# Issuing the prefix products of batch 6 behind the last batch's output projection in the scan stage

## The chip, the cores and the metric

The kernel runs on one core of one Trainium2 chip. The metric is the device time of one execution in microseconds (us); "before" is the median of three runs. Times inside the execution are counted from the start of the span, the stretch from the program's first to its last instruction in the profile.

## What is computed

A block of four residual layers over x of 8 batches x 512 tokens x 256 features, in float32:

```
x = x + scan(layernorm(x))        # silu(x Win), decayed running sum over tokens, times Wout
x = x + ffn(layernorm(x))         # 16 experts, 4 chosen per token, plus 2 shared experts
x = x + attention(layernorm(x))   # 16 heads, causal, scores clipped
x = x + ffn(layernorm(x))         # same weights as the first ffn
```

In `ffn` each token picks 2 of 4 groups of experts and then 4 experts; only these are weighed into its output. The shared experts are computed for every token.

## The kernel before, in words

The kernel works in four stages. A *stretch* (L1315) computes scan or attention for one batch after the other and, beside it, what the following ffn can do early: the layer norm and routing of the batch before, the sorted scatter of its rows to memory, and the shared experts of the batch two back. After a stretch, `routed` (L826) goes through the sorted rows in blocks of 128. There are two stretches and two routed stages: scan, routed, attention, routed. The change touches the first stretch.

**The last iteration of a stretch**, b = 7, runs these pieces side by side (L1379 to L1426):

- `main(7)` (L498): four input projections with the scan (L506 to L522), then the output projection `add_projection` (L452). Its matmuls (L460) come in two halves of two 128-token tiles. Each half fills one bank of the accumulator memory PSUM (`py`), and one VectorE addition (L469) adds it to x. This text calls them half 0 and half 1. Each has 8 matmuls, which the profile shows as 16, since it splits a float32 product into two entries.
- six of the twelve steps of the shared experts of batch 5 (L1031 to L1051); their rest, and the experts of batches 6 and 7, come after the iteration.
- the sends of batch 5: sixteen indirect DMAs from GpSimd (L726), each of which scatters one tile of rows.
- the routing of batch 6, `Route(6)`: normalised rows (L443), their transposes (L403), the logits (L598, moved to SBUF by VectorE at L609), and then the generator `choices` (L621). This yields step by step: group scores, groups, the best four of two tiles, of the other two, and the chosen set `sel` (L668). Then come the *prefix products* (L676 and L677): two small matmuls of `sel` with a triangle and with ones, which count for each token the earlier tokens with the same expert. VectorE adds them to the running counts (`row`, L681, and `where`, L687). The next step makes the *places* of the rows (L693, L699). The one after it makes their *gains* (L709 to L712), which complete batch 6's rows. After that each step is one send (L726); before every second send ScalarE casts two places to integers (L723).

**The order of issue.** `timed(steps, *places)` (L362) gives each step of a piece a place between 0 and 1, and `beside` (L346) always takes the next step of the piece that is least far. `main(7)` counts 10240 columns: its four projections run at 0 to 0.3, and the four tiles of the output projection are issued at 0.6 and 0.7 (half 0) and at 0.8 and 0.9 (half 1). Half 0's addition is issued at 0.8, half 1's at 1.0. Behind this stands a scheduler: it takes the issue order as priority and arranges each engine's instructions by its own model of time. It can let a later instruction pass an earlier one that isn't ready by that model. An engine then runs its instructions in that fixed order, and a waiting instruction holds what is behind it. `tc.issue_after` and `tc.keep_in_program_order` pin single instructions. For batch 6, L675 pins the prefix products behind the last matmul of the six expert steps. The rows of batch 7 (L443) are pinned behind batch 6's gains (L441, L578, L712).

**After the iteration** (L1436 to L1455) follow the rest of batch 5's experts, batch 6's and batch 7's, the other twelve sends of batch 6, and the whole routing of batch 7. That routing needs x of batch 7 after half 1's addition. The counts of batch 7 follow from those of batch 6 (`counts`, L679 to L682). `blocks` (L740) makes the table of blocks. `routed` opens with an `If` (L1012), at which all engines meet.

Of the kernel before, what the change touches and what calls it, by code (L numbers as in the profile page):

```python
# [61 lines left out]
SENT = 4  # L62
# [18 lines left out]
def tile_hybrid_block(  # L81
# [257 lines left out]
    def behind(*pieces):  # L339
        def steps():  # L340
            for piece in pieces:
                yield from piece.steps

        return Piece(sum(piece.columns for piece in pieces), steps())

    def beside(*pieces):  # L346


        def steps():
            done = dict.fromkeys(range(len(pieces)), 0)  # L350
            while done:
                k = min(done, key=lambda k: done[k] / pieces[k].columns)
                step = next(pieces[k].steps, None)
                if step is None:
                    del done[k]
                else:
                    done[k] += step
                    yield step

        return Piece(sum(piece.columns for piece in pieces), steps())  # L360

    def timed(steps, *places):  # L362


        def scaled():
            now = 0
            for place in places:
                yield place - now
                now = place
                next(steps)  # L370
            for _ in steps:
                pass

        return Piece(1, scaled())

    def spread(first: float, last: float, many: int):
        return [first + (last - first) * k / many for k in range(many)]

    def some(steps, many: int):

        for _ in range(many):
            yield next(steps)

    def issue(piece):
        for _ in piece.steps:
            pass
# [85 lines left out]
    class Scan:  # L472
# [3 lines left out]

        norms, scores, choose = (0.08, 0.2, 0.32, 0.4), (0.48, 0.52, 0.61, 0.66), (0.71, 0.97)
        last_rows, last_scores = (0.26, 0.33), (0.43, 0.46)

        def load(self, b: int):  # L480
            if b + 1 < B and b > 0:
                with tc.issue_after(load_x(b + 1).ins):
                    for load in later[b - 1 :: shares]:
                        load()

        def end(self):
            pass
# [598 lines left out]
    class Attention:  # L1086
        mixture, ahead, copies = 1, 2, by_both
        early = 2
        norms, scores, choose = (0.0, 0.12, 0.2, 0.28), (0.42, 0.46, 0.55, 0.6), (0.66, 0.95)
        last_rows, last_scores = (0.2, 0.28), (0.35, 0.38)  # L1090

        def end(self):
            for e in range(first_expert, E):
# [221 lines left out]
    def stretch(layer):  # L1315
# [5 lines left out]
        def norm(b: int, first: bool = False):  # L1321
            def place():
                xn[b] = kb4(f"xn_{i}_{b}")
                return xn[b]

            return normed(b, f"l{i}_{b}", place, first, first)

        def turn(b: int, copies=layer.copies):
            return turned(lambda: xn.pop(b), f"l{i}_{b}", lambda xnT: xT.update({b: xnT}), copies)

        def project(b: int):
            made[b], piece = layer.project(b, xT.pop(b))
            return piece
# [4 lines left out]
        def experts(b: int):  # L1338
            return shared_experts(i, b, lambda: routes.pop(b).held["xnT"], i == 1)
# [31 lines left out]
        def start_route(b: int):  # L1371
            routes[b] = Route(i, b, layer.copies)
            store(b)
            return routes[b]
# [4 lines left out]
        for b in range(1 if begun else 0, B):  # L1379
            pieces = [begun or layer.main(b, made.pop(b))]  # L1380
            begun = None
            nxt, last = b + layer.ahead, b == B - 1
            fill = []
            if layer.ahead > 1 and not last:
                fill.append(project(b + 1))
            if b > 1:
                shared_sum = experts(b - 2)
                if last:

                    each = shared_sum.columns // 12  # L1390
                    rest = Piece((12 - HELD) * each, shared_sum.steps)

                    many = HELD * each if layer.mixture else HELD * each * 3 // 2
                    shared_sum = Piece(many, some(shared_sum.steps, HELD))
                fill.append(shared_sum)
                pieces.append(timed(sends.pop(), 0.1, 0.14, 0.18, *spread(0.22, 0.66 if last else 0.86, NT * TK)))
            if fill:
                pieces.append(behind(*fill))
            if b > 0:
                r = start_route(b - 1)  # L1400
                if last:
                    pieces.append(timed(r.norm(), *spread(0.0, 0.12, NT), *spread(*layer.last_rows, NT)))
                else:
                    first, then, rows, full = layer.norms
                    pieces.append(timed(r.norm(), *spread(first, then, NT), *spread(rows, full, NT)))
                sends.append(r.rest)
                if last:
                    pieces += [
                        timed(r.scores(), *layer.last_scores, *spread(0.5, 0.56, NT)),
                        timed(some(r.rest, PICKS), *spread(0.57, 0.67, PICKS - 1), 0.76),  # L1410
                        timed(some(r.rest, 3 + SENT), 0.79, 0.81, 0.83, *spread(0.85, 1.0, SENT)),
                    ]
                else:
                    pieces += [
                        timed(r.scores(), *layer.scores[:2], *spread(*layer.scores[2:], NT)),
                        timed(some(r.rest, PICKS), *spread(*layer.choose, PICKS)),
                    ]
            if nxt < B:
                added = layer.load(nxt)
                if added is not None:  # L1420
                    pieces.append(timed(added, 0.24, 0.28))
                pieces += [
                    timed(norm(nxt), *spread(0.32, 0.44, NT), *spread(0.56, 0.64, NT)),
                    timed(turn(nxt), 0.75, 0.79),
                ]
            issue(beside(*pieces))  # L1426
            if layer.ahead == 1 and nxt < B:
                issue(project(nxt))
            if i == 0 and b == 2:
                for make in pending:  # L1430
                    make()
# [4 lines left out]
        r = start_route(B - 1)  # L1436
# [20 lines left out]
    with banks_of(one=8):  # L1457
        table = stretch(Scan())
        wqkv_sb, wo_sb = load_attention_weights()
# [6 lines left out]
    with banks_of(one=4, pair=2):  # L1466
        table = stretch(Attention())
# [128 lines left out]
```

## Time and profile before

| what | value |
|---|---|
| median of three runs | 1713.41 us (1713.23, 1713.41, 1718.89) |
| the profiled execution, its own time | 1717.61 us |
| its span | 1715.9 us |
| mean granted TensorE clock | 0.976 |
| TensorE matmul busy | 1612.4 us, 94% of the span |
| VectorE, ScalarE, GpSimd busy | 1146.0, 758.0, 759.9 us |

The page gives busy time by engine (PE is TensorE's matmuls, PEld its weight loads, DVE VectorE, ACT ScalarE, POOL GpSimd, SP the DMA-issuing SyncE). The timeline shows each instruction with its start, its length, and, in brackets, how long its engine stood idle before it and what ended that. "remote" there means a semaphore was raised, but by nothing that the view could name. The ends of matmuls are modelled, not observed. The first routed stage begins at about 367 us, the attention stretch ends at about 1306 us.

### The profile page before, as it was taken

How to read it: one execution, taken by the hardware profiler on the slowest of the kernel's cores; microseconds unless marked ns; L12 is line 12 of the kernel's file. 1: busy time of each engine (PE TensorE's matmuls, PEld its weight loads, DVE VectorE, ACT ScalarE, POOL GpSimd, SP SyncE). 2: the span in 40 equal slices, each digit the busy share in tenths (PEclk: the TensorE clock that was granted, in tenths of full speed). 3: DMA queues.
4: the chain of work that ended last, by engine and by line, in shares of the span. 5: the costliest groups of instructions: out<-in, count | busy, mean ns of one | idle time of the engine just before them, and what ended most of it. 6: DMA issues, size and time to landing. Idle time of an engine off the chain costs nothing.

```text
span 1715.9 us, 34382 instructions
## 1 busy us (share of the span) xinstructions
PE 1612.4 (94%) x10092; PEld 1166.6 (68%) x10092; DVE 1146.0 (67%) x3681; ACT 758.0 (44%) x1506; POOL 759.9 (44%) x656
## 2 busy tenths in 40 slices
PE   6899996999999999999999999999897999999994
PEld 3566663569999999964345445444456999999993
DVE  7977876445666766657877777767753666666663
ACT  3223222135555555545554354454313555555552
POOL 3355553535555655530021431422451555555563
PEclk8999998999999999999999999999998999999997
DMA  4354321547776766540021121122543766677776
GB/s 162 129 180 165 135 96 69 168 104 108 108 104 96 119 103 100 78 93 13 26 70 57 64 80 59 52 75 70 178 159 83 107 96 101 96 138 129 129 127 178
DMA packets 247215, 180.38 MB, mean 105 GB/s; under 512 B 141456, under 2 KB 228272, under 8 KB 247024
## 3 DMA queue, kind: packets, MB, share of 16 engines
q1 hardware_dynamic: 193232, 102.09, 23.5%
q0 software_dynamic: 51984, 72.09, 23.4%
q10 hardware_dynamic: 1808, 3.93, 0.6%
q8 instruction: 86, 1.41, 0.3%
q14 instruction: 105, 0.86, 0.2%
HBM read 81.06 MB, written 96.94 MB: 104 GB/s over the span
## 4 chain that ended last, share of the span: by engine, by line
PE 42%; DVE 6%; DMA 2%; issue 1%; POOL 1%; ACT 1%; ACTq 0%; POOLq 0%; DVEq 0%
PE ph L924 15%; PE pyr L955 7%; PE ps_a L1169 5%; PE po_a L1204 3%; PE pg_m L1031 3%; PE pq_a L1114 3%; PE pd_m L1060 2%; PE py_a L460 2%; PE pv_a L1132 2%; DMA xg<-sorted_m,slots_m 1%; POOL xg L726 1%; DVE w_all L1183 1%; PE pt L906 1%; DVE w_all L1191 1%; DMA part<-rows 1%
## 5 line engine op out<-in xcount | busy, mean ns | idle before, releaser
L965 POOL DMA_INDIRECT part<-rows x272 | 425.6, 1565 | 353.1 <-ACT rows L964 217.0
L726 POOL DMA_INDIRECT xg<-sorted_m,slots_m x256 | 260.1, 1016 | 338.7 <-ACT slots_m L723 84.8
L924 PEld LDWEIGHTS ph<-rows,gate 128*128 128x128 f32 x2160 | 279.1, 192 | 29.3 <-ACT rows L907 17.1
L924 PE MATMUL ph<-rows,gate 128*128 128x128 f32 x2160 | 291.6, 278 | 0.0
L924 PE MATMUL ph<-rows,up 128*128 128x128 f32 x2160 | 285.7, 275 | 0.0
L955 PE MATMUL pyr<-w_all,rows 128*128 x1088 | 278.9, 380 | 0.0
L924 PEld LDWEIGHTS ph<-rows,up 128*128 128x128 f32 x2160 | 263.3, 192 | 0.0
L897 DVE COPY up<-w_all 128x512 f32 x270 | 118.1, 438 | 217.3 <-PE ph L924 188.1
L897 ACT COPY gate<-w_all 128x512 f32 x270 | 166.7, 619 | 115.5 <-DVE up L897 53.6
L955 PEld LDWEIGHTS pyr<-w_all,rows 128*128 128x128 f32 x1088 | 187.0, 192 | 14.4
L964 ACT ACTIVATE rows<-pyr,gain 128x256 f32<-128x256 f32 x272 | 129.0, 474 | 80.2 <-PE pyr L955 58.2
L932 ACT ACTIVATE rows<-ph 128x256 f32<-128x256 f32 x272 | 104.7, 385 | 120.2 <-PE ph L924 100.5
L1180 ACT ACTIVATE w_all<-ps_a 128x1024 f32<-128x1024 f32 x128 | 124.4, 1021 | 57.6 <-PE ps_a L1169 48.2
L934 DVE TENSOR_TENSOR rows<-ph,rows 128x256 f32<-128x256 f32 x272 | 115.2, 423 | 43.8 <-ACT rows L932 37.1
L935 DVE TENSOR_TENSOR rows<-ph,rows 128x256 f32<-128x256 f32 x272 | 115.3, 424 | 26.0 <-issue 1.3
L1031 PE MATMUL pg_m<-xT_m,su_sb 128*128 128x512 f32 x256 | 126.9, 618 | 5.3 <-ACT expert_b L806 5.2
L1169 PE MATMUL ps_a<-w_all 32*128 32x384 f32 (+3 forms) x1024 | 123.0, 478 | 9.0 <-ACT w_all L1180 5.9
L1031 PE MATMUL pg_m<-xT_m,sg_sb 128*128 128x512 f32 x256 | 123.5, 604 | 1.0 <-issue 0.7
L1060 PE MATMUL pd_m<-sd_sb,act_m 128*128 128x256 f32 x512 | 121.4, 382 | 0.9 <-DVE act_m L1051 0.6
L1060 PEld LDWEIGHTS pd_m<-sd_sb,act_m 128*128 128x128 f32 x512 | 95.6, 190 | 25.1 <-issue 7.0
L1169 PEld LDWEIGHTS ps_a<-w_all 32*128 32x128 f32 x1024 | 48.8, 187 | 72.2 <-issue 30.1
L1031 PEld LDWEIGHTS pg_m<-xT_m,su_sb 128*128 128x128 f32 x256 | 46.5, 193 | 64.1 <-issue 51.6
(220 smaller groups left out, 2077.1 us busy)
## 6 DMA issues: line engine op xcount, KB each, us to landing
rows<-xg SPq DMA_DIRECT2D x712, 32.0 KB
rows<-xg SPq DMA_DIRECT2D x94, 134.0 KB
part<-x SPq DMA_DIRECT2D x16, 512.0 KB
part<-ys_m SPq DMA_DIRECT2D x14, 512.0 KB
sum<-part SPq DMA_DIRECT2D x13, 512.0 KB
w_all<-in_L_ffn_gate_w_dram SPq DMA_DIRECT2D x24, 256.0 KB
w_all<-in_L_ffn_up_w_dram SPq DMA_DIRECT2D x24, 256.0 KB
w_all<-in_L_ffn_down_w_dram SPq DMA_DIRECT2D x24, 256.0 KB
```

The costliest lines, as they stand in the source:

```text
L726: nc.gpsimd.indirect_dma_start(out=xg[i], out_offset=bass.IndirectOffsetOnAxis(ap=slots[:, at : at + 1], axis=0), in_=rows[:, t, :], in_of ...
L897: copy(here, w_all[:, bass.ds(held[n][0] + half * KD * F, KD * F)])
L924: nc.tensor.matmul(ph[s][:, f * P : (f + 1) * P], lhsT=both[s][:, k * F + f * P : k * F + (f + 1) * P], rhs=rows[:, ROW + k * P : ROW + (k ...
L934: nc.vector.tensor_mul(act, ph[0], act)
L935: made = nc.vector.tensor_mul(act, ph[1], act)
L955: nc.tensor.matmul(py, lhsT=act[:, f * P : (f + 1) * P], rhs=w_all[:, bass.ds(w + 2 * KD * F + f * D, D)], start=(f == 0), stop=(f == KF - 1),
L964: nc.scalar.mul(y, py, gain[:, TK : TK + 1])
L965: nc.gpsimd.indirect_dma_start(out=parts[i][n % 2], out_offset=bass.IndirectOffsetOnAxis(ap=rows[:, D + 2 * TK : D + 2 * TK + 1].bitcast(U ...
L1031: made = nc.tensor.matmul(dst, lhsT=w[:, k, f * P : (f + 1) * P], rhs=xnT[:, k, :], start=(k == 0), stop=(k == KD - 1),)
L1060: nc.tensor.matmul(py[:, j, :], lhsT=acts[n][:, f, t * P : (t + 1) * P], rhs=shared[n][3][:, f, :], start=(n == 0 and f == 0), stop=(n == ...
L1169: nc.tensor.matmul(ps[j // 2][:, j % 2, col : col + n], lhsT=k_sb[w][r, o, c * P : (c + 1) * P], rhs=q_sb[r, o, c * P : T], start=True, st ...
L1180: nc.scalar.activation(es[two], ps[two][:, :, 0:cols], AF.Exp, scale=ATT_SCALE)
```

## The change

Four places of steps are moved, in the scan stretch alone. The attention stretch gets the same places as before, now from a class attribute.

```diff
 class Scan:
         last_rows, last_scores = (0.26, 0.33), (0.43, 0.46)
+        last_places, last_sends = (0.91, 0.92, 0.93), 0.95
 class Attention:
         last_rows, last_scores = (0.2, 0.28), (0.35, 0.38)
+        last_places, last_sends = (0.79, 0.81, 0.83), 0.85
 stretch, if last:
-                        timed(some(r.rest, 3 + SENT), 0.79, 0.81, 0.83, *spread(0.85, 1.0, SENT)),
+                        timed(some(r.rest, 3 + SENT), *layer.last_places, *spread(layer.last_sends, 1.0, SENT)),
```

For batch 6 in the scan stretch the prefix products go from 0.79 to 0.91, the places from 0.81 to 0.92, the gains from 0.83 to 0.93, and the first four sends with their two casts from 0.85, 0.8875, 0.925 and 0.9625 to 0.95, 0.9625, 0.975 and 0.9875. The step before, which makes `sel`, stays at 0.76. In the issue order the prefix products thus come behind all matmuls of half 1 (0.8 and 0.9). No instruction is added or taken away.

## Prediction

> **What bounds the kernel now.** I read the page, then the waits of the scan stretch, the table of stretches, and the timeline about 281 us. TensorE is the engine to watch:
>
> ```profile
> PE 1612.4 (94%) x10092; PEld 1166.6 (68%) x10092; DVE 1146.0 (67%) x3681; ACT 758.0 (44%) x1506; POOL 759.9 (44%) x656
> ```
>
> It is busy almost everywhere, so a hole in it late in the stretch is worth its length, unless another engine refills it. The waits between 281 and 297 us name the largest one (columns: total, times, longest):
>
> ```profile
> PE pr_m L676 <- DVE sel_m L668: 14.7, 1, 14.7
> DVE x L469 <- remote: 10.0, 1, 10.0
> ```
>
> This is the place the change edits. The table of stretches (busy us of PE, PEld, DVE, ACT, POOL; clock; DMA share; GB/s) shows that nothing replaces it:
>
> ```profile
> 281.00:297.00 16.00, 1.35 (x7) 0.92 (x6) 4.98 (x27) 0.00 (x0) 7.72 (x9) 0.67 0.21 77
> 297.00:312.00 15.00, 15.00 (x60) 11.55 (x60) 9.02 (x38) 1.67 (x7) 8.13 (x10) 0.89 0.54 170
> ```
>
> TensorE works 1.35 of 16 us, and its clock drops to half for part of both stretches. The timeline has the order:
>
> ```profile
> 290.19 0.97 POOL L726 DMA_INDIRECT xg<-sorted_m,slots_m  x1 [0.30 <-issue]
> 292.85 0.69 DVE L469 TENSOR_TENSOR x<-py_s,x 128x512 f32<-128x512 f32 x1 [10.01 <-remote]
> ...
> 295.65 0.58 DVE L668 TENSOR_REDUCE sel_m<-pick_m 128x64 f32<-128x256 f32 x1
> ...
> 296.28 0.69 PE L676 MATMUL pr_m<-sel_m,tri 128*128 128x64 f32 x2 [14.65 <-DVE sel_m L668]
> ...
> 297.19 5.18 PE L460 MATMUL py_s<-w_scan,y_s 128*128 128x256 f32 x16
> ...
> 302.20 1.88 PE L1031 MATMUL pg_m<-xT_m,sg_sb 128*128 128x512 f32 x4
> ```
>
> Half 0 was issued by 281.63. Then TensorE stands at the prefix product, which waits for `sel`. VectorE makes `sel` only after half 0's addition, which stood ahead of it in VectorE's queue and began at 292.85. Half 1 is ready all this time and sits behind the prefix product.
>
> The hole reaches the end: from 302.4 to 366.3 TensorE is short of work for only some 4 us (it is busy 19.71 of 23 us from 312 on, and 24.25 of 25 from 335 on), and then all engines meet at the `If` (TensorE's next matmul, 367.23). So most of what TensorE gains at 302 is kept, if the routing of batch 7 comes early too.
>
> **The unknown term.** Half 0's matmuls end at 281.63 by their rows; the addition that needs nothing but them starts 11.2 us later. Which is right? The Trainium skill (Perfetto Trace Analysis, Tensor Engine Instruction) says that the profiler estimates a matmul's end, while its semaphore rises only when PSUM acknowledges the write. By the rows, the change would save the whole hole; by the waiter, half 0 is released at 292.83 whatever stands behind it. The measured waiter decides for the time before; for the time after it must be bounded:
> - *Below*: prompt. Half 1's rows end at 302.37 and its addition starts at 302.40.
> - *Above*: it stays at 292.83. This hold isn't unique. The waits of VectorE from 60 to 345 us, and the timeline about 314:
>
> ```profile
> DVE logit_m L609 <- remote: 28.9, 6, 9.7
> ```
>
> ```profile
> 313.51 0.64 PE L598 MATMUL pl_m<-xT_m,rw_sb 128*32 128x128 f32 x16
> ...
> 315.61 0.96 POOL L726 DMA_INDIRECT xg<-sorted_m,slots_m  x1 [0.30 <-issue]
> ...
> 318.76 0.32 DVE L609 STREAM_TRANSPOSE logit_m<-pl_m 128x128 f32<-128x128 f32 x1 [9.71 <-remote]
> ```
>
> Batch 7's logits end at 314.15 by their rows and are used at 318.76, though TensorE goes on with other matmuls. Both holds end about 2 us after a run of GpSimd's sends (291.16 to 292.83; 316.57 to 318.76). Further matmuls behind a held one thus don't free it, and batch 5's sends still run to 291.16 after the change. I take the upper end, the row of half 0 itself.
>
> **The change part by part.**
>
> *Half 1 moves ahead of the prefix products.* It runs at 281.6 to 285.1 at full clock (half 0's 16 pieces: 3.6 us). Half 0 is released at 292.83; VectorE adds it (0.69), perhaps half 1's too (0.69), then makes `sel`, which took 292.85+0.69 to 296.23, 2.7 us. So `sel` comes at 296.2 to 296.9; take 296.9. The four prefix pieces take 0.8 (296.28 to half 1's first weight load, 297.09): TensorE is free at 297.7 instead of 302.0. **Gross: 4.3 us.**
>
> *The clock.* Half 1 took 5.18 us because the clock was halved by the hole. The hole stays (285.1 to 296.9), so the same slow stretch falls on the expert matmuls: at 0.89 over 15 us it cost 0.11 x 15 = 1.65. **Minus 1.65; net 2.65.**
>
> *Batch 7's routing.* Half 1's addition comes at about 294 instead of 302.40. From it to the normalised rows (L443, 307.67) it was 5.3 us: 299.5. The rows must also follow batch 6's gains, at 300.50 before and 0.6 later now, 301.2. So they come 6 us earlier, more than TensorE's 2.65. TensorE then waited 2.46 us for batch 7's own `sel` (326.71); that wait goes. **Plus 2.46.** Next late is TensorE's own work to 366.
>
> *Places, gains, four sends, two casts.* Same instructions, some 0.6 us later. On GpSimd nothing is passed: it is idle from 291.16 to 301.56, so sixteen sends at 1.27 us move by 0.6, and batch 7's sends start only at 335.16. On ScalarE the two casts (0.2 each) may now sit before the sigmoid of the next expert matmul (L1049, 304.12), which now comes 2 us after the prefix products' end instead of 7: **0 to 0.6 lost, take 0.6**, since behind that sigmoid wait VectorE's products and TensorE's down matmuls. On SP no DMA is moved, but the load of the attention weights waits for half 1's matmuls (302.40) and the store of x for its addition; both come earlier. Sends kept their 1.27 us beside them, so nothing; if the sends were slowed as at 345.59 (1.39 instead of 0.96), 0.4 us each, under 2 us, hidden in the gap to 335.
>
> *The added wait.* VectorE's first use of the prefix sums now follows half 1; behind it stand only batch 7's statistics, 0.7 us of slack.
>
> Sum: 4.3 - 1.65 + 2.46 - 0.6 = **4.5 us**. It is made in an execution of 1717.61 (span 1715.9 and 1.7 around it), 4.2 above the median. Taken from the median: 1713.4 - 4.5 = **1708.9**; the own range is 1706 to 1712 (the wait for batch 7's `sel` kept or gone, the clock's loss none or double).
>
> **The rivals.**
>
> *A, prompt release.* Half 0's addition starts when VectorE is free, 282.84; `sel` comes at 282.84 + 0.69 + 0.69 + 2.7 = 286.9, the expert matmuls start at 287.7: 14.3 us, with no idle long enough to slow the clock. Batch 6's sends follow batch 5's at once. If batch 7's logits are still held until the twelfth of them has landed (291.8 + 12 x 1.27 + 2 = 309, instead of 318.8), 9.8 remains. 1699 to 1704. For it: half 1 behaves so, and the hole itself could be what delays the release. Against it: the five other holds of L609 with TensorE at work.
>
> *B, no gain.* Batch 7's routing is set by the release of its logits, which ends with the run of sends. The run starts 0.6 later, so it ends 0.6 later, and TensorE waits longer at batch 7's prefix products instead. Or the scheduler, which orders TensorE by its own model, keeps the prefix products between the halves. 1713 to 1714.
>
> *C, slower.* Before, the sends paused at 316.57 after twelve, because the seventh cast stood behind a held copy on ScalarE; the pause let the logits go at 318.76. If the casts now come in time, sixteen sends run from 302.2 to 302.2 + 16 x 1.27 = 322.5, and the logits go at 324.7: batch 7's `sel`, which came 7.8 us after them, comes at 332.5, 5.9 us later than before. It decides from the point where the thirteenth send starts without a pause. 1719.3; up to 11.2 (the longest hold) if the logits wait still longer, 1724.6.
>
> **How the numbers follow.** Forecast 0.42, A 0.25, B 0.17, C 0.16. A measurement of this kernel tells about 0.5%, 8.6 us, from no change. Faster by more: A, 0.25, and 0.02 of the forecast. Slower by more: the upper half of C, 0.08. The rest, 0.65, is within. The range runs from 1699.0, A's fast end, to 1719.5, C's near end; some 0.06 lies below and 0.08 above.
>
> **What would show it.** In the changed profile TensorE has no L676 between two L460 groups. The forecast wants half 1's rows near 282 to 285, half 0's addition still near 292.8 with some 10 us of "remote", the expert matmuls near 297.7, and the wait for batch 7's `sel` gone. A wants that addition before 285. B wants batch 7's logits used at 318 to 320; C, at 324. I am wrong altogether if TensorE's 15 us hole appears elsewhere ahead of 366, or if the `If` comes later although 302 came earlier.

## The result

The changed kernel is slower. Its median is 1721.59 us, that of the kernel before 1717.36 us in the same runs (22 each): a ratio of 1.003, with an interval of 1.0019 to 1.0040, or about 4.2 us. The forecast was 4.5 us faster. On a chip that releases TensorE's products at once, the same change came out 2.4 us faster (0.9986, 0.9972 to 1.0001), which isn't quite clear of no change; this dependence is the main finding below.

The profiled execution took 1726.32 us (span 1724.6, mean clock 0.973). Line numbers from L480 on are one higher than before (L676 is now L677), and in the experiments some are higher still. This trace is 2.0 us late already at half 0 (280.00 instead of 278.01), ahead of all that the change touches, so times are compared from half 0 on.

The page's row of TensorE, then the table of stretches (busy us of PE, PEld, DVE, ACT, POOL; clock; DMA share; GB/s):

```profile
PE 1617.2 (94%) x10092; PEld 1168.8 (68%) x10092; DVE 1146.5 (66%) x3681; ACT 757.2 (44%) x1506; POOL 756.8 (44%) x656
```

```profile
281.00:297.00 16.00, 6.08 (x29) 5.00 (x27) 5.58 (x32) 0.00 (x0) 9.41 (x10) 0.77 0.29 97
297.00:312.00 15.00, 13.52 (x48) 9.26 (x49) 9.39 (x44) 2.70 (x10) 3.84 (x4) 0.79 0.39 131
312.00:335.00 23.00, 12.94 (x48) 6.43 (x47) 9.03 (x44) 2.70 (x7) 11.73 (x13) 0.83 0.28 101
```

TensorE's share of the whole kernel is 94% before and after. The stretches tell more: TensorE works 6.08 of the first 16 us instead of 1.35, and 12.94 of the last 23 instead of 19.71. The hole has moved. The timeline of the first part:

```profile
280.00 7.07 PE L460 MATMUL py_s<-w_scan,y_s 128*128 128x256 f32 x32
...
294.95 0.69 DVE L469 TENSOR_TENSOR x<-py_s,x 128x512 f32<-128x512 f32 x1 [10.11 <-remote]
...
297.75 0.58 DVE L669 TENSOR_REDUCE sel_m<-pick_m 128x64 f32<-128x256 f32 x1
298.25 0.68 DVE L469 TENSOR_TENSOR x<-py_s,x 128x512 f32<-128x512 f32 x1
298.48 0.66 PE L677 MATMUL pr_m<-sel_m,tri 128*128 128x64 f32 x2 [11.40 <-DVE sel_m L669]
299.36 1.17 PE L1032 MATMUL pg_m<-xT_m,sg_sb 128*128 128x512 f32 x1
```

Half 0 (the first 16 of the 32 entries at 280.00; rows' end 283.62) is still released 11.3 us late, and the expert products start at 299.36, which is 4.8 us earlier than before when counted from half 0. This far it went as forecast. The second part of the same timeline shows batch 6's gains, its first send, an expert product of batch 6 (the one from su_sb, which VectorE reads at L1052), batch 7's logits, the thirteenth send, and batch 7's prefix products:

```profile
303.12 0.60 ACT L1050 ACTIVATE sig_m<-pg_m 128x512 f32<-128x512 f32 x1 [22.30 <-PE pg_m L1032]
303.75 0.69 DVE L1051 TENSOR_TENSOR sig_m<-pg_m,sig_m 128x512 f32<-128x512 f32 x1 [1.16 <-ACT sig_m L1050]
304.36 0.16 DVE L710 TENSOR_REDUCE den_m<-choices_sm 128x4 f32<-128x16 f32 x1
306.11 0.17 DVE L713 SCALAR_TENSOR_TENSOR sorted_m<-choices_sm,den_m 128x16 f32<-128x16 f32 x1
307.17 0.96 POOL L727 DMA_INDIRECT xg<-sorted_m,slots_m  x1 [14.02 <-DVE off_m L432]
...
315.46 1.88 PE L1032 MATMUL pg_m<-xT_m,su_sb 128*128 128x512 f32 x4
...
318.53 0.32 DVE L610 STREAM_TRANSPOSE logit_m<-pl_m 128x128 f32<-128x128 f32 x1 [9.34 <-PE pg_m L1032]
...
322.45 0.96 POOL L727 DMA_INDIRECT xg<-sorted_m,slots_m  x1 [0.30 <-issue]
...
328.41 0.69 DVE L1052 TENSOR_TENSOR act_m<-pg_m,sig_m 128x512 f32<-128x512 f32 x1 [5.03 <-remote]
...
332.55 0.66 PE L677 MATMUL pr_m<-sel_m,tri 128*128 128x64 f32 x2 [10.06 <-DVE sel_m L669]
```

The kernel before has the gains, the thirteenth send and batch 7's prefix products at these times:

```profile
300.50 0.17 DVE L712 SCALAR_TENSOR_TENSOR sorted_m<-choices_sm,den_m 128x16 f32<-128x16 f32 x1
...
319.55 0.97 POOL L726 DMA_INDIRECT xg<-sorted_m,slots_m  x1 [2.98 <-ACT score_m L613]
...
326.71 0.41 PE L676 MATMUL pr_m<-sel_m,tri 128*128 128x64 f32 x2 [2.46 <-DVE sel_m L668]
```

Three things to see. The gains (L713) end at 306.3; before they ended at 300.7. In VectorE's queue they now stand behind an expert product (L1051) that waits for ScalarE. The send at 322.45 is the thirteenth, and it starts 0.3 us behind the twelfth: the pause of before (2.98 us) is gone. And the expert product at 315.46, whose rows end at 317.34, reaches VectorE only at 328.41, 11.1 us later and 1.2 us behind the last send's end (327.21). VectorE stands idle for the last 5.03 us of that, and behind this product in its queue stands batch 7's chosen set. TensorE waits 10.06 us for that, instead of 2.46.

Counted from half 0, the first expert product ends 3.0 us earlier than before, batch 7's prefix products start 3.85 us later, and the stretch's last expert product ends 4.56 us later (372.86 less 280.00, against 366.31 less 278.01). That accounts for the measured loss of about 4.2 us.

### The profile page after: what moved, and what is told of

It reads as the page before. It is cut to its first block, busy times and chain, and to the rows that moved or that the text cites. A ratio compares the mean times of both kernels' runs of the same rounds, so it can differ in the third digit from the quotient of the medians.

```text
span 1724.6 us, 34386 instructions
## 1 busy us (share of the span) xinstructions
PE 1617.2 (94%) x10092; PEld 1168.8 (68%) x10092; DVE 1146.5 (66%) x3681; ACT 757.2 (44%) x1506; POOL 756.8 (44%) x656
## 4 chain that ended last, share of the span: by engine, by line
PE 42%; DVE 6%; DMA 3%; issue 2%; POOL 1%; ACT 1%; POOLq 0%; ACTq 0%; DVEq 0%
PE ph L925 14%; PE pyr L956 7%; PE ps_a L1171 5%; PE po_a L1206 3%; PE pg_m L1032 3%; PE pq_a L1116 3%; PE pd_m L1061 2%; PE pv_a L1134 2%; PE py_a L460 2%; DMA xg<-sorted_m,slots_m 1%; DMA part<-rows 1%; POOL xg L727 1%; DVE w_all L1185 1%; PE pt L907 1%; DVE w_all L1193 1%
```

## The experiments

Two words are used below. A *hold* is the time from the end of a product's rows to its release, where an engine stands idle for it at the end. A *session* is a group of up to four runs on one chip. Each session from B on had a chip of its own; which chip A had isn't on record. Each ratio is to the kernel before in the same session, with its 95% interval in brackets. The edits are shown shortened.

| session | runs | kernel before, median us | half 0's addition behind its rows' end, us | holds |
|---|---|---|---|---|
| A | before, after | 1717.36 | 11.2 and 11.3 | yes |
| B | E1 to E4 | 1720.60 | 12.1 to 12.3 (E2 to E4) | yes |
| C | E5 to E8 | 1692.88 | 0.0 (E5) | none |
| D | E9 to E12 | 1693.96 | 0.0 | none |
| E | E13, E14 | 1694.14 | 0.0 (E13) | none |
| F | E15, E16 | 1725.22 | 12.1 (E15) | yes |
| G | E17, E18 | 1718.82 | (rests in both) | yes, in batches without rests |

**E1: batch 5's sends moved out of the hole (B).**

```diff
-    tc.keep_in_program_order(nc.scalar.copy(slots[:, pair], places[:, pair]))
+    if i == 0 and b == B - 3:
+        with tc.issue_after(added[f"s{B - 1}", 0].ins):   # half 0's addition
+            nc.vector.tensor_copy(slots[:, pair], places[:, pair])
-    spread(0.22, 0.66, NT * TK)
+    spread(0.82, 0.9, NT * TK)
```

> The changed kernel, with batch 5's sixteen sends moved out of TensorE's hole: their casts go to VectorE, behind half 0's addition, so no send can start before half 0 has been released. Theory (a run of sends holds back the release of TensorE's finished products): half 0's addition starts within 1 us of half 0's rows' end instead of 7.9 to 11.2 us behind it, and TensorE's wait for batch 6's chosen set falls from 11.4 us to under 5. Rival (the hold is TensorE's own, set off by its standing at a wait): the addition still comes 8 us or more behind the rows, the wait stays near 11. The time: the sends of batch 5 now run at about 285 to 305 and those of batch 6 behind them, so new holds may take back what the hole gave: ratio to before 0.996 to 1.003.

Timeline of E1:

```profile
281.70 0.69 DVE L469 TENSOR_TENSOR x<-py_s,x 128x512 f32<-128x512 f32 x1
284.00 1.03 POOL L732 DMA_INDIRECT xg<-sorted_m,slots_m  x1 [24.60 <-DVE slots_m L727]
284.96 0.36 PE L678 MATMUL pr_m<-sel_m,tri 128*128 128x64 f32 x2
...
323.96 0.32 DVE L611 STREAM_TRANSPOSE logit_m<-pl_m 128x128 f32<-128x128 f32 x1 [16.59 <-remote]
```

With no send in flight half 0's addition starts 0.03 us behind its rows' end (281.67), and TensorE's wait for batch 6's chosen set, 11.4 us, is gone. The theory is right on this: without the sends there is no hold. The ratio is 1.0014 (0.9990 to 1.0039): 28 sends then run without a break from 284.0 to 319.3, batch 7's rows wait for them (TensorE stands 13.2 us at their transposes), and its logits are held 8.2 us.

**E2: the gains ahead of the expert product (B).**

```diff
-    nc.vector.tensor_mul(sig, ph, sig)
+    with tc.issue_after(gained[b + 1].ins) if b == B - 3 and b + 1 in gained else nullcontext():
+        nc.vector.tensor_mul(sig, ph, sig)
```

> The changed kernel, with one thing pinned: VectorE makes batch 6's gains ahead of the expert product that waits for ScalarE's sigmoid (in the changed kernel they stand behind it). Theory (the change loses because batch 6's gains, and so its sends and batch 7's rows, come late): gains near 303.5 instead of 306.3, first send of batch 6 near 304.3 instead of 307.2, batch 7's chosen set and the end of the stretch about 3 us earlier than in the changed kernel; ratio to before 1.000 to 1.001. Rival 1 (the loss is TensorE's halved clock, which now falls on the expert products): the clock is the same, nothing is gained, 1.0025. Rival 2 (the run of sends only begins earlier, and holds something else): the gains come earlier, the end doesn't, 1.0025.

Timeline of E2:

```profile
324.82 0.32 DVE L610 STREAM_TRANSPOSE logit_m<-pl_m 128x128 f32<-128x128 f32 x1 [16.41 <-remote]
...
332.65 0.66 PE L677 MATMUL pr_m<-sel_m,tri 128*128 128x64 f32 x2 [10.48 <-DVE sel_m L669]
```

The gains end at 303.8 and the first send starts at 304.8, as expected; the time isn't better (1.0036, 1.0020 to 1.0051). Fourteen sends now run unbroken to 322.3, and the logits are held 11.4 us, to 324.8. Rival 2 is right: late gains alone are not the loss. What costs is an unbroken run of sends on top of a product that batch 7's routing needs, whichever product that is.

**E3: batch 6's last eight sends behind batch 7's chosen set (B).**

```diff
+    if i == 0 and b == B - 2 and at >= 8:
+        with tc.issue_after(made_sel[0, B - 1].ins):
+            nc.vector.tensor_copy(slots[:, pair], places[:, pair])
-    *spread(0.0, 0.5, NT * TK - SENT)
+    *spread(0.0, 0.2, 4), *spread(0.525, 0.555, 8)
```

> The changed kernel, with a pause put into batch 6's sends: the casts for the last eight are made by VectorE behind batch 7's chosen set, so these sends can't run while that set is made. Theory (the unbroken run of sixteen sends holds an expert product that VectorE waits for ahead of batch 7's chosen set): VectorE's 5.0 us wait at the expert product is gone or under 2 us, TensorE waits under 4 us for batch 7's chosen set instead of 10.1, the stretch ends 6 to 7 us earlier than in the changed kernel: ratio to before 0.999 (0.998 to 1.000). Rival (the hold comes from TensorE's standing at the prefix products, not from the sends): the wait stays near 5 us and the time near the changed kernel's, 1.002 to 1.004.

Timeline of E3 (L1074 copies a down product of the shared experts whose rows ended at 341.03):

```profile
326.60 0.41 PE L678 MATMUL pr_m<-sel_m,tri 128*128 128x64 f32 x2 [3.96 <-DVE slots_m L727]
...
355.89 0.96 POOL L732 DMA_INDIRECT xg<-sorted_m,slots_m  x1 [0.30 <-issue]
360.97 0.58 ACT L1074 COPY ys_m<-pd_m 128x512 f32<-128x512 f32 x1 [12.88 <-remote]
```

The chosen set comes at 326.5 instead of 332.4 and VectorE's 5.0 us wait is gone, as the theory said; the time is far off (1.0091, 1.0055 to 1.0127, expected 0.998 to 1.000). The eight and batch 7's sixteen now run without a break from 326.8 to 356.9, and the down product is held 19.9 us, to 4 us behind the run. The length of a run doesn't set the hold alone: in E1 a product that ended inside a run of 28 was held 8.2 us.

**E4: half 0's addition behind batch 6's chosen set (B).**

```diff
+    first = tag == f"s{B - 1}" and half == 0
+    with tc.issue_after(made_sel[0, B - 2].ins) if first else nullcontext():
         nc.vector.tensor_add(rows, py, rows)
```

> The changed kernel, with half 0's addition pinned behind batch 6's chosen set in VectorE's queue. Theory (the chosen set is late only because it stands behind the held addition; the hold itself doesn't depend on it): the chosen set comes at about 287, TensorE's 11.4 us wait falls under 1.5 us, the addition itself still starts at 293 to 295; TensorE's clock isn't halved at 297 to 312. Batch 6's gains come at about 300 instead of 306.3, since TensorE's expert products are done long before. Ratio to before 0.994 to 0.998, if the later holds don't grow. Rival (another wait takes the hole's place, since VectorE still stands 8 us at the addition and the expert products wait for VectorE): hole of 5 us or more between 288 and 300, ratio 0.998 to 1.002.

Timeline of E4, with VectorE's steps to the chosen set:

```profile
285.62 0.09 DVE L657 MATCH_VALUE_LOAD which_m<-best_m,s_m 128x8 f32 x1 [2.04 <-remote]
...
288.50 0.58 DVE L672 TENSOR_REDUCE sel_m<-pick_m 128x64 f32<-128x256 f32 x1 [1.00 <-DVE pick_m L664]
...
289.32 0.66 PE L680 MATMUL pr_m<-sel_m,tri 128*128 128x64 f32 x2 [4.64 <-DVE sel_m L672]
...
293.55 0.69 DVE L471 TENSOR_TENSOR x<-py_s,x 128x512 f32<-128x512 f32 x1 [4.47 <-remote]
...
327.63 0.66 PE L680 MATMUL pr_m<-sel_m,tri 128*128 128x64 f32 x2 [9.62 <-DVE sel_m L672]
```

The addition is held as before, but the chosen set no longer is: TensorE's first wait falls from 11.40 to 4.64 us, though not under the 1.5 us expected. The ratio is 1.0010 (0.9993 to 1.0027), not 0.994 to 0.998: TensorE waits 9.62 us for batch 7's chosen set (327.5). What it saves early it waits away there, for behind that wait stand some 40 us of its own work in before, after, E2 and E4 alike (last expert product less chosen set: 39.7, 40.5, 40.9, 40.4). In these four traces the stretch ends when batch 7's chosen set says so.

The first two rows hold a surprise. VectorE waits there for its own instruction of just before, 2.04 and 1.00 us. So it isn't only TensorE's products that are late.

**E5, E6 (C) and E13 (E): rests in the sends of batches 5 and 6.** Behind every fourth send GpSimd does two small instructions on four numbers per partition. E6 has E4's edit besides. E13 is E5 again.

```diff
+    if i == 0 and b in (B - 3, B - 2) and at % 4 == 3:
+        for _ in range(2):
+            rests.append(nc.gpsimd.tensor_tensor(scratch, scratch, neg_half, ALU.pow))
+            tc.keep_in_program_order(rests[-1])
```

> The changed kernel, with the sends of batches 5 and 6 broken up in place: after every fourth send GpSimd does two small instructions on a scratch tile (about 2 us). Nothing else is moved. Theory (a finished product of TensorE isn't released while GpSimd's sends follow each other without a break, and the end of the stretch is batch 7's chosen set plus 40 us): half 0's addition starts in the first rest behind its rows' end, within 6 us instead of 7.9 to 11.2, TensorE's first wait falls under 7 us; batch 7's logits are used within 4 us of their rows' end; batch 7's chosen set comes 3 to 7 us earlier than the changed kernel's 332.4, and the end with it: ratio to before 0.998 to 1.001. Rival (the release comes only when the whole queue of sends has landed, rests or not): the holds are as long as the stretched runs of sends, 4 us longer than now, ratio 1.004 or more.

> The kernel with half 0's addition behind batch 6's chosen set, and the sends of batches 5 and 6 broken up by 2 us after every fourth. Theory: TensorE's first wait stays under 5 us, its 9.6 us wait for batch 7's chosen set falls under 5, since the chosen set comes at 320 to 324 instead of 327.5: the end is some 40 us behind it, ratio to before 0.995 to 0.998. Rival (the chosen set is held by ScalarE and VectorE's work for the expert products, not by the sends): it stays at 327, ratio 1.001.

> The changed kernel with 2 us rests after every fourth send of batches 5 and 6, again, since the chip it ran on showed no holds. Theory: where there are holds, half 0's addition starts in the first rest behind its rows' end, within 6 us instead of 7.9; batch 7's logits within 4 us; batch 7's chosen set comes 3 us or more before the changed kernel's 332.4; ratio 0.997 to 1.001. Rival (the release comes only when all sends have landed, rests or not): 1.004 or more. Where there are no holds: 1.001 again, since the rests only delay batch 7's rows.

Ratios 1.0009 (0.9998 to 1.0021), 1.0019 (1.0005 to 1.0034), 1.0011 (0.9998 to 1.0025). They could not show what they were made for: on these chips nothing is held at all, with or without rests, and the kernel before is 23 to 32 us faster than in A, B, F and G. The rests only delay batch 7's rows (TensorE waits 7.0 us for them in E5).

**E7 (C), E11 (D), E14 (E), E15 (F): batch 7's prefix products later, with E4's edit.**

```diff
-    *spread(0.36, 0.68, chain), *spread(0.7, 1.0, 8)
+    *spread(0.36, 0.56, PICKS), 0.74, 0.76, 0.78, *spread(0.8, 1.0, 8)
```

> The kernel with half 0's addition behind batch 6's chosen set, and batch 7's prefix products issued later, behind two more expert products of batch 6, so that TensorE stands less at them. Theory (what TensorE saves at 289 to 297 is waited away at batch 7's prefix products, because these stand too early in its queue): the 9.6 us wait falls by the length of the products put ahead, 2 to 4 us each, and the end with it: ratio to before 0.995 to 0.999. Rival (TensorE can't run ahead, since its accumulator banks aren't drained while the products' releases are held): the wait only changes its name, ratio 1.001.

> The kernel that gave 0.9973 (half 0's addition behind batch 6's chosen set, batch 7's prefix products behind two more expert products), again, beside the changed kernel. Where there are no holds: 0.996 to 0.9985 again. Where there are: TensorE's 9.6 us wait at batch 7's prefix products falls to 6 or less, ratio 0.995 to 0.999.

> The kernel with half 0's addition behind batch 6's chosen set and batch 7's prefix products behind two more expert products, again, for a chip with holds. There TensorE's 9.6 us wait at batch 7's prefix products falls to 6 or less, ratio 0.995 to 0.999 (rival: the accumulator banks aren't drained during the hold, 1.001). Without holds: 0.996 to 0.9985 as twice before.

> The kernel with half 0's addition behind batch 6's chosen set and batch 7's prefix products behind two more expert products, for a chip with holds if it is one. There: TensorE's second wait (9.6 us without the later prefix products) falls to 6 or less, 0.995 to 0.999; if the accumulator banks aren't drained during the hold, 1.001. Without holds: 0.996 to 0.998 as three times before.

Without holds 0.9973 (0.9960 to 0.9985), 0.9973 (0.9961 to 0.9986) and 0.9967 (0.9955 to 0.9978): faster than the kernel before. Whether it is faster than the changed kernel too isn't clear (E11's 0.9973 and E9's 0.9986 in session D have intervals that overlap). With holds (E15) 0.9993 (0.9975 to 1.0010), no difference: the second wait is 3.51 us instead of 9.62, as expected, but batch 7's sends then hold the block table's product 9.6 us. In the timeline of E7, VectorE takes the same two steps as in E4 without any wait:

```profile
282.63 0.09 DVE L657 MATCH_VALUE_LOAD which_m<-best_m,s_m 128x8 f32 x1
...
283.58 0.58 DVE L672 TENSOR_REDUCE sel_m<-pick_m 128x64 f32<-128x256 f32 x1
```

Batch 5's sends run under these rows too (270.98 to 291.2). The sends are the same; the sessions differ.

**E8 (C): E4's edit on the kernel before.**

> The kernel before, with half 0's addition pinned behind batch 6's chosen set: the prefix products stay between the halves. Theory (the order of prefix products and half 1 isn't what matters once the chosen set no longer stands behind the held addition): TensorE's 14.7 us wait falls under 6 us, batch 7's chosen set comes within 2 us of the 326.6 of before, so TensorE waits 8 us or more for it instead of 2.5, and the time is within 0.2% of before, like that of the changed kernel with the same pin (1.001). Rival (the hole's length counts at the end): ratio 0.995 or less.

0.9997 (0.9983 to 1.0011). The ratio is the expected one, but its reason isn't: without holds TensorE never waits for batch 7's chosen set, and the pinned addition changes little, since it was prompt. On a chip with holds this kernel wasn't run.

**E9, E10, E12 (D): the changed kernel, the kernel before, and the changed kernel with E7's later prefix products alone, on one chip.**

> The changed kernel as it is, to see it on the same chip as the three runs beside it. In the runs with rests (and in the two beside them) no product of TensorE was held at all, whether sends ran or not, while in all traces taken earlier each run of sends held some. Theory (the hold belongs to the chip on which the run is made, and the change's effect turns on it): where half 0's addition starts within 0.1 us of half 0's rows' end, the change gains, since TensorE's wait for batch 6's chosen set (2.6 us with the prefix products between the halves) goes: ratio 0.998 to 1.000; where the addition comes 8 us or more late, it loses as before: 1.002 to 1.004. Rival (the absence of holds came from the edits): the holds are there as before, and the ratio is 1.003, though the time of the kernel before is near 1692.

> The kernel before as it is, for its trace on the same chip. Theory (the hold belongs to the chip): its half 0 is released as in the changed kernel beside it, promptly or late in both. If promptly: TensorE waits 2 to 3 us for batch 6's chosen set instead of 14.7, and not at all for batch 7's.

> The changed kernel with batch 7's prefix products issued later, and half 0's addition left where it was. Where there are no holds the pinned addition can't matter, so the same as the kernel with both, 0.996 to 0.9985. Where there are, TensorE's first wait stays at 11 us, its second (10.1 us) falls to 6 or less: ratio 0.998 to 1.001.

Timeline of E10, the kernel before:

```profile
283.46 0.69 DVE L469 TENSOR_TENSOR x<-py_s,x 128x512 f32<-128x512 f32 x1
...
286.89 0.69 PE L676 MATMUL pr_m<-sel_m,tri 128*128 128x64 f32 x2 [3.47 <-DVE sel_m L668]
...
287.80 5.97 PE L460 MATMUL py_s<-w_scan,y_s 128*128 128x256 f32 x16
```

Timeline of E9, the changed kernel:

```profile
279.89 7.07 PE L460 MATMUL py_s<-w_scan,y_s 128*128 128x256 f32 x32
283.54 0.69 DVE L469 TENSOR_TENSOR x<-py_s,x 128x512 f32<-128x512 f32 x1
...
287.07 0.41 PE L677 MATMUL pr_m<-sel_m,tri 128*128 128x64 f32 x2
...
297.58 1.41 PE L403 MATMUL pt_m<-ident,sorted_m 128*128 128x128 f32 x8 [2.94 <-DVE sorted_m L443]
```

Here half 0 is released at once in both. The change does what it says: the wait of 3.47 us is gone, half 1 runs at full clock (in E10 it took 5.97 us instead of 3.6), and 2.94 us are given back in a wait for batch 7's rows. 3.47 + 2.4 - 2.94 = 2.9 us; the last expert product ends 2.6 us earlier, and the ratio is 0.9986 (0.9972 to 1.0001), 2.4 us, not quite clear of no change. TensorE's wait in E10 was 3.47 us, more than the 2 to 3 expected. E12 gave 0.9991 (0.9976 to 1.0007), less than expected: there TensorE waits 3.43 us for batch 7's rows, in E11 1.63. Why E4's edit helps there wasn't tried further.

**E16 (F): E5's kernel, now on a chip with holds.**

> The changed kernel with 2 us rests after every fourth send of batches 5 and 6, for a chip with holds if it is one. There: half 0's addition within 6 us of its rows' end, batch 7's logits within 4, batch 7's chosen set 3 us or more before 332.4, 0.997 to 1.001; if only the end of all sends releases, 1.004 or more. Without holds: 1.001 as twice before.

Timeline of E16 (L740 is the rest):

```profile
281.66 0.69 DVE L469 TENSOR_TENSOR x<-py_s,x 128x512 f32<-128x512 f32 x1
...
283.12 2.17 POOL L740 TENSOR_TENSOR scratch<-scratch,neg_half 128x4 f32<-128x4 f32 x2
...
353.58 0.80 PE L1069 MATMUL pd_m<-sd_sb,act_m 128*128 128x256 f32 x1 [6.47 <-DVE act_m L1060]
```

0.9950 (0.9930 to 0.9970): 8.6 us faster than before, where the same kernel cost 0.1% twice without holds. Half 0's addition comes 0.04 us behind its rows, batch 7's logits 0.7 us behind theirs (4.6 to 11.4 in A and B). The theory holds in this: with the sends in fours the holds of half 0 and the logits are gone. It isn't the break itself that releases half 0, for its rows end 3.4 us into a run of four sends (278.26 to 283.10) and it is released inside that run. What is left (6.47 us) lies behind batch 7's sends, which have no rests here.

**E17, E18 (G): the parts that gained, together.** E4's and E7's edits, and rests in batches 5, 6 and 7: two small instructions (E17) or one (E18).

> The parts that gained put together: half 0's addition behind batch 6's chosen set, batch 7's prefix products behind two more expert products, and a 2 us rest after every fourth send of batches 5, 6 and 7. On a chip with holds: the holds of 4 to 11 us behind batch 7's sends, which rests for batches 5 and 6 alone left (TensorE's 6.5 us wait at the down products and the late block table), are gone; ratio 0.990 to 0.995. On a chip without: the rests cost as much as the later prefix products gain, 0.998 to 1.001. Rival (batch 7's sends, which end 8 us later, become the bound of the next stage): 0.996 or more with holds, 1.002 without.

> The same with rests of 1 us. If a break of 1 us is enough for a release: as good or better than 2 us on a chip with holds (0.990 to 0.995), and better without them (0.996 to 0.999). If it is too short: half 0's addition is held 8 us again on a chip with holds, and the ratio there is 0.999 as without rests.

0.9956 (0.9942 to 0.9969) and 0.9920 (0.9896 to 0.9944). In E17 the rival came true in part: the next stage waits 7.1 us for rows from batch 7's sends, which now end at 355. One instruction, of 1.04 us in most of the rests, is rest enough: in E18 no idle engine waits over 0.6 us for a held product in this part, and the `If` comes 72.6 us behind half 0. That is what a chip without holds takes for the kernel before (72.2, E10); with holds it took 89.2. E18 is the fastest version measured on a chip with holds; on one without it hasn't run, and rests of two instructions cost 0.1% there. A rest also lowers the mean rate of sends, from one in 1.27 us to one in some 1.5 us (E18), and no run tells whether the break or the rate is what counts.

## Why the prediction was wrong

*Half 1 ahead: right.* The chosen set came at 298.3, 296.3 without the trace's 2.0 us, against 296.2 to 296.9 forecast; the expert products at 297.4 against 297.7.

*The clock: right.* The first expert product took 3.7 us instead of 1.9; 1.8 lost against 1.65. Net 3.0 us against 2.65. The 0.6 us for ScalarE's casts weren't lost: the sigmoid starts at 303.12, 0.04 us behind its product, and the casts come after it.

*Batch 7's routing, "Plus 2.46": the step that failed.* It said that the gains come 0.6 us later, the rows 6 us earlier, and that the wait for batch 7's chosen set goes. The gains came 3.6 us later (5.6 by the traces' own clocks), the rows 1.9 us earlier, and the wait grew by 7.6 us. Two things were missed. The planner put the gains behind the waiting expert product; the forecast had kept VectorE's order as it was and named only batch 7's statistics behind the added wait. And the run of sends, with no pause left in it, went with a hold of 11.1 us on an expert product that VectorE had to take ahead of batch 7's chosen set. E2 shows that the second weighs more: counted from half 0, its gains came 2.0 us earlier than in the changed kernel, and the wait was still 10.48 us.

*The kept gain.* "Most of what TensorE gains at 302 is kept, if the routing of batch 7 comes early too": the condition decides. In E4, counted from half 0, the first expert product ended 9.8 us earlier than before, and TensorE then waited 9.62 us for batch 7's chosen set instead of 2.46; the last expert product ended 2.0 us later than before.

*Rivals C and B: right that batch 7's chosen set would come late, not in the product held.* The thirteenth send started without a pause, as C said. But both let the logits set the loss, and in the changed kernel these were used at 318.53, in the middle of the run and, counted from half 0, 2.2 us earlier than before; what came late was the expert product behind them. C's two numbers, logits at 324.7 and chosen set at 332.5, are close to E2's 324.8 and 332.5 and to the changed kernel's chosen set at 332.4. That is in part luck: C let sixteen sends start at 302.2, while the run began at 307.2 in the changed kernel and at 304.8 in E2, where it had fourteen, and the traces' clocks are 1.5 to 2.0 us apart. C's price, 5.9 us, was 4.6 in this trace: counted from half 0 the chosen set came 3.8 us later, and 0.7 more was lost behind the new wait, part of it by the clock (the next expert product took 3.73 us instead of 3.37).

*Rival A, prompt release: true on other chips, with another sum.* It let the hold vanish in the changed kernel only, and so counted 14.3 us. Where the release is prompt, it is prompt before the change too, and the wait to be saved is 3.5 us. The rule that a matmul's end in the profile is an estimate (Trainium skill, Perfetto Trace Analysis, Tensor Engine Instruction) doesn't account for the hold either: E1 and E10 have the same matmuls with their ends within 0.04 us of their release.

## What to carry to other kernels

A "remote" wait on a product whose rows have ended is a question, not a cost of that product: look for what else runs from its end to its release, and move that. Match the wait with the product that the instruction really reads: here the rows of three later products ended before the release too. Before counting a saved wait, find the wait further on that stands on the same chain; here the saved time was waited away at batch 7's prefix products. A change in the order of issue moves every queue that the planner arranges, so read the other engines' order as well, and let a small edit be judged on more than one chip.

## What the runs showed of the hardware

- *Semaphores are raised late while indirect sends follow each other*, in four of the seven sessions. It strikes TensorE's products (up to 19.9 us in E3) and VectorE's waits for its own last instruction (2.04 and 1.00 us in E4, none in E7).
- *The lag grows within a run of sends.* In the changed kernel six products of TensorE end one after the other from 313.71 to 322.49; the raw events of the trace have their semaphores at 318.50, 321.35, 328.39, 329.81, 329.87 and 329.93, with the last send's end at 327.21. Early in a run there is none: in E1 a product that ends 5 us into the run of 28 is released within 0.02 us. With a rest of one instruction (mostly 1.04 us) behind every fourth send no idle engine waits over 0.6 us (E18).
- *The sessions differ.* In three of seven nothing was held; the kernel before takes 1693 to 1694 us there, and 1717 to 1725 in the others. Each session from B on had its own chip, so the chip and the hour can't be told apart.
- *Not settled* is what holds the semaphores. The traces with holds also lack records of semaphores: the raw events have 23,653 to 24,647 of them in the ten traces with holds and 34,273 to 34,346 in the ten without. The same kernel has 24,502 in session A and 34,343 in E9, with 34,386 records of instructions in both. Of the sixteen marks of landing that each send leaves in E8, most sends of the traces with holds have fewer than ten. That fits a crowded path for semaphores, but no run tested it. It also leaves a rival open: every time given here comes from an execution that the profiler recorded too, so the holds may come with the recording of semaphores, and what the kernels take unrecorded isn't known.
